# A two-layer graph network on one core: two more PSUM banks for the products of the list, and one table of columns

## The chip, the core and the metric

The kernel runs on one core of one Trainium2 chip. The metric is the device time of one execution in microseconds; the kernel before has a median of 3094.66 us over 3 runs (3094.16 to 3096.91). The engines have the names of the profile: PE is TensorE (PEld its weight loads), DVE is VectorE, ACT is ScalarE, POOL is GpSimd, SP is SyncE.

## The reference

The input is a graph with 12500 nodes of 128 features and 200000 edges sorted by target. Each edge has a relation, 0 to 9, the argmax of ten of its attributes. A layer takes for each target node and relation the mean of the source nodes' features, multiplies it by that relation's 128 x 128 matrix, sums over relations, and adds the node's own features times a root matrix and a bias:

```python
seg = dst * NUM_REL + edge_type
sums = segment_sum(x[src], seg, N * NUM_REL)
cnt = segment_sum(ones, seg, N * NUM_REL)
mean = (sums / maximum(cnt, 1)[:, None]).reshape(N, NUM_REL, -1)
layer = einsum('nrd,rdo->no', mean, w_rel) + x @ root + bias
```

There are two such layers, with a relu between them. The result is the layer norm of x plus the second layer's output.

## The kernel before

Edges are handled in tiles of 128. For a tile, POOL gathers the 128 source rows from DRAM (`gathered`, L749). DVE builds a one-hot matrix, 128 edges by (relation, node within a window of w nodes), by comparing a table of column numbers with one key per edge (`ones`, L757). ACT scales it by each edge's weight (`weighted`, L755). PE multiplies the gathered rows by the one-hot (the placement product, L976 in layer 1 and L1479 in layer 2) into a PSUM bank. DVE adds the bank into `cc`, a ring of sums in SBUF, at an offset read from a register (`sum_into`, L790). When all edges of a block of nodes are in, PE projects the block: ten products with the relations' matrices and one with what is there already (`projected`, L737 and L740). ACT copies it (L1413), PE transposes it (L1420), and DVE and ACT normalise it and store it (`normed`, L698 to L710). ACT clears the ring behind it (`cleared`, L720), and at the start of each lap of the ring DVE adds its overhang into it (`folded`, L727).

Layer 1 goes through all edges and, for edges whose source is finished already, does layer 2's share as well. What is left for layer 2 is, first, 166 tiles at the start (the plain bunches), and then a list of the edges that layer 1 had to skip. The list is put together on the chip during the plain bunches (`brought_together`, `listed`), in `mask`, a PSUM tile with the name "go" of three banks, and in one half of the ring, which is cleared again afterwards; from then on `ready` holds "ring". The list has 709 tiles.

In layer 2 a bunch is one product bank: several tiles of the same window, or one tile, or one piece of at most 48 of a wider window (up to 120 nodes). The loop at L1450 writes every engine's order out by hand (nothing is rescheduled). Iteration p issues:

- the one-hot of bunch p+4 on DVE (AH is 4) and the weighting of bunch p+3 on ACT. There are six one-hot buffers, so a one-hot waits for the product six bunches before its own;
- the gathers of bunch p on POOL, eight rows of tiles to a buffer, with seven buffers (GB);
- the products of bunch p on PE, into a bank of the pool `ps_y`, which has three;
- due steps of the list's making;
- the additions of bunch p-2 on DVE (BE is 2);
- if a block is now complete, its projection; and the later steps of earlier blocks (transposes, normalisation, clearing) that are due by the count of tiles gathered. Once all tiles are gathered, a block's steps follow each other at once.

The eight PSUM banks are: two for projections and transposes (`ps_f`), three for the products (`ps_y`), three for `mask`. After the list is built, `mask` holds three tables of column numbers (for pieces that begin at columns 0, 48 and 96) and small helpers.

Waits between engines come from the framework: an instruction waits for the earlier ones whose tile it overwrites or reads.

Of the kernel before, what the change touches and what calls it, by code (L numbers as in the profile page):

```python
# [9 lines left out]
F32 = mybir.dt.float32  # L10
# [3 lines left out]
ALU = mybir.AluOpType  # L14
# [6 lines left out]
P = 128  # L21
NREL = 10
EMB = 16
RS = 32
WN = 12
KW = NREL * WN
WZ = 48
WMAX = 120
# [14 lines left out]
YB = 512  # L43
# [20 lines left out]
def rgcn_resnorm_kernel(ctx: ExitStack, tc: tile.TileContext, x, src, dst, attr, w_rel1, root1, b1,  # L64
# [7 lines left out]
    nc = tc.nc  # L72
# [35 lines left out]
    def finished_in(k):  # L108

        return -(-done_after(k) // QB) - 1 + BEHIND  # L110
# [4 lines left out]
    ER = RT * P  # L115
# [3 lines left out]
    for k in range(K0, K1 + 1):  # L119
        r = max(0, -(-(QB * (finished_in(k) + READY) - T0) // RT))  # L120
# [33 lines left out]
    def rows_at(u, at):  # L154

        rs = [r for r, (lo, hi) in at.items() if lo < u * P + P and hi > u * P]
        return (min(rs), max(rs)) if rs else (max(at), max(at))
# [7 lines left out]
    for l, (a, last) in enumerate(((0, SPLIT), (SPLIT, NR))):  # L165
        while a < last:
            b = a + 1
# [9 lines left out]
            a = b  # L177
# [55 lines left out]
    def chunk_rows(c):  # L233
        return min(CT, NT - c * CT)
# [109 lines left out]
    n = chunk_rows(NCH - 1)  # L344
# [402 lines left out]
    def gathered(g, j, table, idx, n):  # L747

        nc.gpsimd.indirect_dma_start(out=g[:, j * C:(j + n) * C], out_offset=None, in_=table,  # L749
                                     in_offset=bass.IndirectOffsetOnAxis(ap=idx, axis=0))  # L750

    def weighted(oh, j, m, w):

        s = oh[:, j * m:(j + 1) * m]
        nc.scalar.activation(s, s, AF.Copy, scale=w)  # L755

    def ones(keys, cols, n, w):  # L757

        oh = dpool.tile([P, YB], F32, name="oh")
        m = NREL * w  # L760
        o = oh[:, :n * m]
        if w == WN:
            nc.vector.tensor_tensor(o.rearrange("p (t m) -> p t m", m=m), cols[:, None, :m].to_broadcast([P, n, m]),  # L763
                                    keys[:, :, None].to_broadcast([P, n, m]), op=ALU.is_equal)
        else:
            nc.vector.tensor_tensor(o.rearrange("p (t r n) -> p t r n", r=NREL, n=w),  # L766
                                    cols[:, None, :, :w].to_broadcast([P, n, NREL, w]),
                                    keys[:, :, None, None].to_broadcast([P, n, NREL, w]), op=ALU.is_equal)
        return oh

    def offsets(row, t0, n, limits):
# [270 lines left out]
    ps_y = fast.enter_context(tc.tile_pool(name="ps_y", bufs=3, space=PSUM))  # L1042
# [7 lines left out]
    mask = ps_m.tile([P, 3 * YB], I32, name="go")  # L1050
    iotaM = mask[:, P + ER - KW:P + ER].bitcast(F32)
    nc.vector.tensor_copy(iotaM, columns[:, :KW])
    tables = {WN: iotaM}
# [3 lines left out]
    def brought_together(ready, first):  # L1057

        EW = P + ER
# [19 lines left out]
        tri, wide = flat[:, at:at + P], flat[:, at + P:at + P + NREL * WZ].rearrange("p (r n) -> p r n", n=WZ)  # L1079
# [15 lines left out]
        for a in range(0, RT, 4):  # L1095
            pt = ps_f.tile([P, YB], F32, name="pf")
            n = min(RT - a, 4)
# [43 lines left out]
        for s in range(11):  # L1141
# [11 lines left out]
            c = max(m, KW)  # L1153
# [8 lines left out]
        for a, b, t in ((0, KW, gl[:, :KW]), (KW, EW, go)):  # L1162
            q = t.bitcast(F32)
# [2 lines left out]
            nc.vector.scalar_tensor_tensor(v[:, a:b], d0[:, a:b], 0.5, q, op0=ALU.is_gt, op1=ALU.mult)  # L1166
        nc.vector.scalar_tensor_tensor(A, d0, 0.5, A, op0=ALU.is_gt, op1=ALU.mult)
        yield 1
        for c in range(0, WMAX, WZ):
            w = min(WZ, WMAX - c)  # L1170
            t = mask[:, c * NREL:(c + w) * NREL].bitcast(F32).rearrange("p (r n) -> p r n", n=w)
            nc.vector.tensor_scalar(t, wide[:, :, :w], float(c), None, op0=ALU.add)
            tables[c, WZ] = t
        assert WMAX * NREL <= ER
        n = -(-NT2 // P)
        assert sorted(first) == list(range(n))
        hots = [t[:, :EW].rearrange("r (c t) -> r c t", t=P) for t in (X, Y)]
# [2 lines left out]
        def put(i, c):  # L1180

            u0, u1 = c * P, min(NT2, c * P + P) - 1
            p = u1 + 1 - u0
            m = max(-(-(P - 1 + cap_of[r]) // P) for r in range(rows_at(u0, extent[u0 >= UX])[0], rows_at(u1, extent[u1 >= UX])[1] + 1))
            assert m * P <= EW
            o = WMAX * NREL + i * (EW // P)
            assert o + EW // P <= EW - KW
            qc = mask[:, o:o + EW // P].bitcast(F32)
            nc.vector.tensor_scalar(qc[:NR, :m], columns[:NR, :m], f[:NR, 3:4], -float(u0), op0=ALU.add, op1=ALU.add)
            hot = hots[i % 2]  # L1190
            nc.vector.tensor_tensor(hot[:, :m], columns[:NR, None, :].to_broadcast([NR, m, P]),
                                    qc[:NR, :m, None].to_broadcast([NR, m, P]), op=ALU.is_equal)
            pp = ps_f.tile([P, YB], F32, name="pf")
            for j in range(m):
                nc.tensor.matmul(pp[:p, :2 * P], hot[:, j, :p], both[:, :, j * P:(j + 1) * P], start=(j == 0), stop=(j == m - 1))  # L1195
            nc.scalar.activation(packed[:p, c], pp[:p, :2 * P], AF.Copy)

        put(0, first[0])
        yield 1
        head = listed(first[0])  # L1200
# [87 lines left out]
    def layer_2():  # L1288
# [16 lines left out]
        bunches = [(0, False, t, min(QB, T0 - t), WN, 0, WN) for t in range(0, T0, QB)]  # L1305
# [135 lines left out]
        busy = 0  # L1441
        flag = None
        gs, ohs, zps, offs = {}, {}, {}, {}
        AH, BE = 4, 2
        i = 0
        ready = set()
        wanted = list(dict.fromkeys(c for _, second, t0, n, *_ in bunches if second for c in (t0 // P, (t0 + n - 1) // P)))
# [2 lines left out]
        for p in range(-AH, NB + BE):  # L1450
            if p + AH < NB:
                l, second, t0, n, w, c, _ = bunches[p + AH]
                keys = keyB if second else keyE
                assert not second or {t0 // P, (t0 + n - 1) // P} <= ready
                ohs[p + AH] = ones(keys[:, t0:t0 + n], tables[(c, WZ) if second else WN], n, w)
            if 0 <= p + AH - 1 < NB:
                l, second, t0, n, w, c, _ = bunches[p + AH - 1]
                for j in reversed(range(n)):
                    weighted(ohs[p + AH - 1], j, NREL * w, (wB if second else wE)[:, t0 + j:t0 + j + 1])
            if p == -AH:  # L1460
                jobs.run(0)
            if p < 0:
                continue
            if p < NB:
                l, second, t0, n, w, c, whole = bunches[p]
                oh = ohs.pop(p)
                zp = zps[p] = ps_y.tile([P, YB], F32, name="zp")
                if not c:
                    for j in range(n):
                        if made % GQ == 0:  # L1470
                            g = gpool.tile([P, GQ * C], F32, name="g")
                        gs[second, t0 + j] = g, made % GQ
                        made += 1
                        idx = (idxB if second else idxE)[:, t0 + j:t0 + j + 1]
                        gathered(g, gs[second, t0 + j][1], hD, idx, 1)
                m = NREL * w
                for j in range(n):
                    gt, b = gs[second, t0 + j]
                    nc.tensor.matmul(zp[:, j * m:(j + 1) * m], gt[:, b * C:(b + 1) * C], oh[:, j * m:(j + 1) * m],  # L1479
                                     start=True, stop=True)  # L1480
                    if c + w == whole:
                        del gs[second, t0 + j], gt
                i = issued[p + 1]
            if flag is None and i >= NG - 8 * QB:
                flagged()
                flag = 0
            jobs.run(i)
            q = p - BE
            if q >= 0:
                l, second, t0, n, w, c, whole = bunches[q]  # L1490
                assert not l or "ring" in ready
                for j in range(n):
                    t = t0 + j
                    if (second, t) not in offs:
                        if second:
                            m = min(GB2, (UX, NT2)[l] - t)
                            assert {t // P, (t + m - 1) // P} <= ready
                            vals = offsets(rowB[:, t:t + m], t, m, bounds2)
                        else:
                            m = min(GB2, T0 - t)  # L1500
                            if t % CT == 0:
                                row = rows_.tile([1, CT], I32, name="row")
                                nc.scalar.dma_start(row, b_i[t // CT:t // CT + 1, :])
                            vals = offsets(row[:, t % CT:t % CT + m], t, m, bounds)
                        offs = {k: v for k, v in offs.items() if k[0] and (k[1] >= UX) != l}
                        offs.update({(second, t + d): v for d, v in enumerate(vals)})
                    ring = 1 - l
                    sum_into(slice(ring, ring + 1), zps[q], j * NREL * w, offs[second, t], w, c)
                del zps[q]
            while due and due[0][0] <= q + 1 and (i >= busy or i >= NG or clear[due[0][1]] and i + 2 >= free_until(due[0][1])):  # L1510
                k = due.pop(0)[1]
                finish(k, i)
                ended.add(k)
                busy = i + (13 if block(k)[1] > YB * 5 // 8 else 9)
            todo.run(i)
# [173 lines left out]
```

## Time and profile before

| | |
|---|---|
| median of 3 runs | 3094.66 us |
| profiled execution: time, span | 3098.4 us, 3096.6 us |
| mean granted TensorE clock | 0.823 |
| PE busy | 2427.0 us, 78% |
| DVE busy | 1989.1 us, 64% |
| ACT busy | 1292.9 us, 42% |
| POOL busy | 2308.9 us, 75% |
| first gather of layer 2 | 1971.1 us |
| last gather | 3065.2 us |

Times in the profile are counted from the start of the span. Busy time leaves out register and semaphore work and the issuing of DMAs. Each row of a group has the line, engine, operation and shapes, then busy time, mean ns of one, and the idle time of its engine just before it, with what ended it; "issue" there means that the profile names no cause. A row of a timeline has the start, the time taken and, in brackets, the idle time before it. A row of a stretch has its bounds and length, the busy time and count of each engine in it (PE, PEld, DVE, ACT, POOL in this order, those that have any), the granted TensorE clock, the share of the DMA engines, and GB/s. An fp32 product shows as two PE records.

### The profile page before, as it was taken

How to read it: one execution, taken by the hardware profiler on the slowest of the kernel's cores; microseconds unless marked ns; L12 is line 12 of the kernel's file. 1: busy time of each engine (PE TensorE's matmuls, PEld its weight loads, DVE VectorE, ACT ScalarE, POOL GpSimd, SP SyncE). 2: the span in 40 equal slices, each digit the busy share in tenths (PEclk: the TensorE clock that was granted, in tenths of full speed). 3: DMA queues.
4: the chain of work that ended last, by engine and by line, in shares of the span. 5: the costliest groups of instructions: out<-in, count | busy, mean ns of one | idle time of the engine just before them, and what ended most of it. 6: DMA issues, size and time to landing. Idle time of an engine off the chain costs nothing.

```text
span 3096.6 us, 39943 instructions
## 1 busy us (share of the span) xinstructions
PE 2427.0 (78%) x10905; PEld 1805.4 (58%) x10905; DVE 1989.1 (64%) x5272; ACT 1292.9 (42%) x3006; POOL 2308.9 (75%) x2450
## 2 busy tenths in 40 slices
PE   2768887888888888888888899646577787777887
PEld 2546666566666566666666667545555555555665
DVE  7875746465656565555555554598677677677676
ACT  3543333333333333333333334322445555555453
POOL 7777777777777777777777777677777777777774
PEclk8768888888888878787888789856788999988888
DMA  7865445454545454545454444322222222222222
GB/s 210 233 204 173 143 124 159 120 163 123 163 119 163 121 162 124 162 123 162 123 161 124 127 121 120 101 58 63 60 70 74 73 74 74 74 74 73 74 73 59
DMA packets 260631, 371.57 MB, mean 120 GB/s; under 512 B 49654, under 2 KB 189467, under 8 KB 260404
## 3 DMA queue, kind: packets, MB, share of 16 engines
q0 software_dynamic: 100368, 251.49, 29.5%
q1 hardware_dynamic: 106339, 91.83, 9.6%
q10 hardware_dynamic: 53697, 25.62, 2.8%
q8 instruction: 94, 1.54, 0.2%
q14 instruction: 133, 1.09, 0.1%
HBM read 323.78 MB, written 57.76 MB: 123 GB/s over the span
## 4 chain that ended last, share of the span: by engine, by line
PE 37%; POOL 18%; issue 16%; DVE 13%; DMA 11%; ACT 3%; DVEq 1%; ACTq 0%; POOLq 0%; SPq 0%
POOL g L749 18%; PE pf L737 16%; DMA g<-XH,idxE 10%; PE zp L976 9%; PE zp L1479 8%; DVE cc L790 4%; DVE oh L766 2%; PE pf L740 1%; ACT cc L720 1%; ACT oh L755 1%; DVE cc L1157 1%; PE pf L1195 1%; DVEq L775 1%; DVE oh L763 1%; DVE go L1145 1%
## 5 line engine op out<-in xcount | busy, mean ns | idle before, releaser
L749 POOL DMA_INDIRECT g<-XH,idxE x1397 | 1321.7, 946 | 425.6 <-issue 383.9
L790 DVE TENSOR_TENSOR cc<-cc,zp 128x240 f32 (+16 forms) x2507 | 962.9, 384 | 719.7 <-PE zp L976 503.1
L976 PE MATMUL zp<-oh,g 128*128 128x120 f32 x5920 | 1053.4, 334 | 323.6 <-DMA g<-XH,idxE 230.5
L976 PEld LDWEIGHTS zp<-oh,g 128*128 128x128 f32 x5920 | 926.1, 236 | 482.4 <-issue 187.1
L749 POOL DMA_INDIRECT g<-hD,idxB x709 | 670.2, 945 | 216.1 <-issue 202.7
L755 ACT ACTIVATE oh<-oh,wE 128x120 f32<-128x120 f32 x1729 | 530.2, 383 | 640.8 <-DVE oh L763 557.3
L1479 PE MATMUL zp<-oh,g 128*128 128x120 f32 (+18 forms) x1888 | 514.8, 417 | 256.8 <-DVE cc L790 102.3
L737 PE MATMUL pf<-cc,w 128*128 128x256 f32 (+6 forms) x2120 | 691.4, 485 | 30.3 <-DVE cc L790 21.3
L1479 PEld LDWEIGHTS zp<-oh,g 128*128 128x128 f32 x1888 | 346.1, 230 | 401.8 <-issue 252.2
L737 PEld LDWEIGHTS pf<-cc,w 128*128 128x128 f32 x2120 | 411.8, 208 | 279.6 <-issue 205.0
L755 ACT ACTIVATE oh<-oh,wB 128x150 f32<-128x150 f32 (+18 forms) x778 | 342.6, 483 | 293.7 <-DVE oh L766 276.6
L766 DVE TENSOR_TENSOR oh<-go,keyB 128x480 f32<-128x480 f32 (+14 forms) x478 | 262.9, 550 | 132.8 <-PE zp L1479 131.6
L720 ACT ACTIVATE cc<-zero 128x2560 f32<-128x2560 f32 (+4 forms) x188 | 322.0, 1717 | 21.7 <-DVE cc L790 19.6
L763 DVE TENSOR_TENSOR oh<-bank,keyE 128x480 f32<-128x480 f32 x391 | 253.2, 648 | 0.0
L670 ACT ACTIVATE a<-pf,b 128x512 f32<-128x512 f32 (+1 forms) x27 | 17.3, 639 | 453.6 <-PE pf L740 453.6
L749 POOL DMA_INDIRECT g<-hD,idxE x166 | 158.4, 954 | 62.6 <-issue 46.6
L749 POOL DMA_INDIRECT g<-in_x_dram,idxE x166 | 157.0, 946 | 52.3 <-issue 47.2
L546 DVE TENSOR_TENSOR eqb<-bank,kh 128x1344 bf16<-128x1344 f32 (+2 forms) x65 | 100.5, 1549 | 2.3 <-PE pf L557 1.9
L555 PE MATMUL pf<-eqb,identb 128*128 128x512 bf16 (+2 forms) x130 | 64.7, 498 | 11.6 <-DVE eqb L546 11.4
L882 ACT ACTIVATE v<-pf,b 128x512 f32<-128x512 f32 (+2 forms) x29 | 18.0, 619 | 120.1 <-PE pf L740 100.5
L557 PE MATMUL pf<-eqb,identb 128*128 128x512 bf16 (+2 forms) x130 | 64.1, 493 | 0.0
L415 DVE SCALAR_TENSOR_TENSOR reach<-u,reach 128x6 f32<-128x6 f32 x252 | 42.2, 167 | 7.4
(235 smaller groups left out, 991.5 us busy)
## 6 DMA issues: line engine op xcount, KB each, us to landing
m<-in_edge_attr_dram SPq DMA_DIRECT2D x48, 672.0 KB
g<-XH,idxE POOLq DMA_INDIRECT x1397
XH<-in_x_dram ACTq DMA_DIRECT2D x24, 512.0 KB
XH<-zero ACTq DMA_DIRECT2D x24, 512.0 KB
g<-hD,idxB POOLq DMA_INDIRECT x709
XH<-hb SPq DMA_DIRECT2D x43, 256.0 KB
out_dram<-o SPq DMA_DIRECT2D x47, 128.0 KB
xb<-in_x_dram SPq DMA_DIRECT2D x23, 256.0 KB
```

Of the source, the lines that this page charges most:

```text
L546: nc.vector.tensor_tensor(eq[:p], kpP[:p, None, :R].to_broadcast([p, DB, R]), fore, op=ALU.is_equal)
L555: nc.tensor.matmul(pc[:p], identb[:p, :p], eq[:p, k:k + 4, L:], start=(d + k == 1), stop=False)
L557: nc.tensor.matmul(pc[:p], identb[:p, :p], back, start=False, stop=(d + k + 3 == L))
L720: nc.scalar.activation(cc[:, l, h * H:(h + 1) * H, o:o + n], zero[:, None, :n].to_broadcast([P, H, n]), AF.Copy)
L737: nc.tensor.matmul(po[:, :n], wsb[l][:, r, :], cc[:, l if ring is None else ring, r, o:o + n], start=(r == 0), stop=False)
L749: nc.gpsimd.indirect_dma_start(out=g[:, j * C:(j + n) * C], out_offset=None, in_=table, in_offset=bass.IndirectOffsetOnAxis(ap=idx, axis=0))
L755: nc.scalar.activation(s, s, AF.Copy, scale=w)
L763: nc.vector.tensor_tensor(o.rearrange("p (t m) -> p t m", m=m), cols[:, None, :m].to_broadcast([P, n, m]), keys[:, :, None].to_broadcast([ ...
L766: nc.vector.tensor_tensor(o.rearrange("p (t r n) -> p t r n", r=NREL, n=w), cols[:, None, :, :w].to_broadcast([P, n, NREL, w]), keys[:, :, ...
L790: nc.vector.tensor_tensor(s, s, z, op=ALU.add)
L976: nc.tensor.matmul(zp[:, a + l * KW:a + (l + 1) * KW], g[:, (slot[j] + l) * C:(slot[j] + l + 1) * C], oh[:, j * KW:(j + 1) * KW], start=Tr ...
L1479: nc.tensor.matmul(zp[:, j * m:(j + 1) * m], gt[:, b * C:(b + 1) * C], oh[:, j * m:(j + 1) * m], start=True, stop=True)
```

## The change

In the list part, once "ring" is ready, bunches go around five banks in place of three: those with p % 5 of 3 or 4 use the second and third bank of `mask`. The additions of the list are issued three bunches behind the products (BE is 3), those of the plain bunches two behind as before. So that the two banks are free, one table of 48 columns, in the first bank of `mask`, replaces the three: for a piece that begins at column c, the one-hot's comparison adds c in the same instruction (a scalar-tensor-tensor form in place of the tensor-tensor form).

```diff
-    def ones(keys, cols, n, w):
+    def ones(keys, cols, n, w, c=0):
...
-            nc.vector.tensor_tensor(o.rearrange("p (t r n) -> p t r n", r=NREL, n=w),
-                                    cols[:, None, :, :w].to_broadcast([P, n, NREL, w]),
-                                    keys[:, :, None, None].to_broadcast([P, n, NREL, w]), op=ALU.is_equal)
+            to = o.rearrange("p (t r n) -> p t r n", r=NREL, n=w)
+            a = cols[:, None, :, :w].to_broadcast([P, n, NREL, w])
+            b = keys[:, :, None, None].to_broadcast([P, n, NREL, w])
+            if c:
+                assert n == 1
+                nc.vector.scalar_tensor_tensor(to[:, 0], a[:, 0], float(c), b[:, 0], op0=ALU.add, op1=ALU.is_equal)
+            else:
+                nc.vector.tensor_tensor(to, a, b, op=ALU.is_equal)
...
-        for c in range(0, WMAX, WZ):
-            w = min(WZ, WMAX - c)
-            t = mask[:, c * NREL:(c + w) * NREL].bitcast(F32).rearrange("p (r n) -> p r n", n=w)
-            nc.vector.tensor_scalar(t, wide[:, :, :w], float(c), None, op0=ALU.add)
-            tables[c, WZ] = t
-        assert WMAX * NREL <= ER
+        assert WZ * NREL <= YB
+        tables[WZ] = mask[:, :WZ * NREL].bitcast(F32).rearrange("p (r n) -> p r n", n=WZ)
+        nc.vector.tensor_copy(tables[WZ], wide)
...
-            o = WMAX * NREL + i * (EW // P)
+            o = WZ * NREL + i * (EW // P)
...
-        AH, BE = 4, 2
+        AH, BE = 4, 3
+        plain = sum(not b[1] for b in bunches)
...
-                ohs[p + AH] = ones(keys[:, t0:t0 + n], tables[(c, WZ) if second else WN], n, w)
+                ohs[p + AH] = ones(keys[:, t0:t0 + n], tables[WZ if second else WN], n, w, c)
...
+            five = p >= plain and "ring" in ready
...
-                zp = zps[p] = ps_y.tile([P, YB], F32, name="zp")
+                if p % 5 > 2 and five:
+                    b = p % 5 - 2
+                    zp = mask[:, b * YB:(b + 1) * YB].bitcast(F32)
+                else:
+                    zp = ps_y.tile([P, YB], F32, name="zp")
+                zps[p] = zp
...
-            q = p - BE
-            if q >= 0:
+            q = p - (BE if five else BE - 1)
+            if q in zps:
```

## The prediction

> **What bounds the kernel now.** I began with the busy time by stretches, to see where the changed code runs: the list part of layer 2, from about 2200 us to the end. Then came the waits of the stretch 2250 to 3065, then its groups, then the timeline of a few bunches and of the end. The first four rows below are busy times by stretch; the last two count, from the first gather of layer 2 to 2500 us, the gathers and the records of the placement products. A row of waits gives total us, times, and longest us.
>
> ```profile
> 2000.00:2100.00 100.00, 46.92 (x199) 40.08 (x197) 95.97 (x172) 29.83 (x83) 75.93 (x80) 0.61 0.23 60
> 2100.00:2200.00 100.00, 64.16 (x291) 54.68 (x291) 72.02 (x179) 38.02 (x98) 75.69 (x80) 0.74 0.23 58
> 2300.00:2500.00 200.00, 159.63 (x573) 103.17 (x571) 140.64 (x379) 108.00 (x208) 151.24 (x161) 0.91 0.28 73
> 2250.00:3065.00 815.00, 645.07 (x2510) 466.72 (x2511) 586.74 (x1624) 433.04 (x894) 616.39 (x652) 0.89 0.28 73
> 1971.00:2500.00 529.00, 400.28 (x423) 0.77 0.27 70
> 1971.00:2500.00 529.00, 218.89 (x806) 148.42 (x806) 0.77 0.27 70
> ```
> ```profile
> POOL g L749 <- issue: 186.2, 611, 0.3
> DVE oh L766 <- PE zp L1479: 129.0, 52, 6.2
> PE zp L1479 <- issue: 59.0, 25, 3.1
> PE zp L1479 <- DVE cc L790: 52.7, 39, 4.8
> DVE cc L790 <- PE pf L737: 35.2, 8, 5.8
> PE zp L1479 <- DMA g<-hD,idxB: 4.1, 6, 1.1
> ```
> ```profile
> L1479 PE MATMUL zp<-oh,g 128*128 128x150 f32 (+16 forms) x1471 | 424.7, 427 | 156.3 <-issue 59.0 <-DVE cc L790 52.7 <-PE zp L1479 12.8
> L766 DVE TENSOR_TENSOR oh<-go,keyB 128x480 f32<-128x480 f32 (+15 forms) x462 | 253.4, 548 | 130.2 <-PE zp L1479 129.0 <-PE pf L1230 0.3
> L737 PE MATMUL pf<-cc,w 128*128 128x256 f32 (+4 forms) x860 | 209.0, 402 | 16.9 <-DVE cc L790 8.4 <-DVE cc L727 8.2
> ```
>
> POOL issues gathers at an even pace (616.39 us busy plus 186.2 us of 0.3 us gaps in 815), so it looks like the bound. But the products do not keep up with it: up to 2500 us there are 423 gathers and 806/2 = 403 products, two records each, so PE is 20 gathers (25 us) behind, and it waits for a gather only 4.1 us in all. The seven g buffers hold 56 gathers, so this lag holds nobody; it decides the end, though, because PE must still work it off. What PE and DVE do together is therefore the chain of this part. POOL is a floor close beneath it.
>
> DVE waits for PE 129.0 + 35.2 = 164.2 us. There are 860/20 = 43 projections of a block and 462 bunches, so one block is 815/43 = 18.95 us, 10.7 bunches, and 3.8 us of DVE waiting. Nearly all the waiting lies behind a projection, as these rows show: the projection, the first product after it, and the one-hot it releases.
>
> ```profile
> 2606.46 5.81 PE L737 MATMUL pf<-cc,w 128*128 128x256 f32 x20
> 2612.53 1.96 PE L1479 MATMUL zp<-oh,g 128*128 128x480 f32 x10
> 2613.54 0.66 DVE L766 TENSOR_TENSOR oh<-go,keyB 128x480 f32<-128x480 f32 x1 [5.30 <-PE zp L1479]
> ```
>
> Elsewhere DVE runs without a pause. DVE's own work is thus 18.95 - 3.8 = 15.1 us per block; with about 3 us for a block's normalisation (3.1 in the rows of the end below), one iteration of DVE is (15.1 - 3)/10.7 = 1.13 us. Two kinds of iteration, one-hot and additions, in rows: 1.29 us with two tiles of 24 columns, 1.44 with three of 15.
>
> ```profile
> 3041.90 0.65 DVE L766 TENSOR_TENSOR oh<-go,keyB 128x480 f32<-128x480 f32 x1
> 3042.47 0.81 DVE L790 TENSOR_TENSOR cc<-cc,zp 128x230 f32 x2
> 3043.19 0.65 DVE L766 TENSOR_TENSOR oh<-go,keyB 128x480 f32<-128x480 f32 x1
> ...
> 2603.64 0.62 DVE L766 TENSOR_TENSOR oh<-go,keyB 128x450 f32<-128x450 f32 x1
> 2604.17 0.99 DVE L790 TENSOR_TENSOR cc<-cc,zp 128x150 f32 x3
> 2605.08 0.65 DVE L766 TENSOR_TENSOR oh<-go,keyB 128x480 f32<-128x480 f32 x1
> ```
>
> **The change, part by part.** One table: three operations that wrote 480, 480 and 240 columns become one copy of 480; each took 0.58 us, so about 1.2 us of DVE goes, once, in the stage that builds the list. I take it as nothing: bounds 0 and -1.2 us. For pieces beyond the first (69 of them: 944 products for 875 gathers), the one-hot adds its offset in a scalar-tensor-tensor form. No such row of 480 elements exists; the nearest has 1408 in 1675 ns, or 0.57 for 480 if proportional, against 0.65 for the plain form. Bounds 69 x (-0.08 to +0.08) = -6 to +6 us; I take 0, as it is the same work per element.
>
> ```profile
> L1172 DVE TENSOR_SCALAR go<-cc 128x480 f32<-128x480 f32 (+1 forms) x3 | 1.7, 578 | 0.1
> L1103 DVE SCALAR_TENSOR_TENSOR cc<-cc,seen_below,go 127x1408 f32<-127x1408 int32 x1 | 1.7, 1675 | 0.0
> ```
>
> Five banks, additions three behind. By the text of the kernel, the product of bunch p now needs the addition of p-5 where it needed p-3, and the 52.7 us (and probably the 59.0 us without a named cause) of PE's waits would shrink. But the two added banks are cut from the tile "go", whose first bank holds the table that every one-hot reads, and the built order of the changed kernel shows what that makes of the waits. Of 190 products into these two banks, 188 wait for the one-hot of p+4, issued just ahead of them; and where the bunch before wrote into one of these banks, the one-hot of p+4 waits for the product of p-1 (185 times) where it waited for p-2. So in two iterations of each five DVE and PE run in lock step: one-hot, product, one-hot. Nothing in the banks demands this, but it is in the program.
>
> One lock step costs DVE: one-hot 0.65, then 0.09 until the product starts (addition's end 3052.18 + 0.83, product at 3053.10), then 1.02 from the product's start to the next one-hot (3060.84 to 3061.86), 1.76 in all where the iteration lasted 1.29: 0.47 us. With three tiles of 15: 0.62 + 0.09 + 1.02 - 1.44 = 0.29. I take 0.4.
>
> ```profile
> 3052.18 0.83 DVE L790 TENSOR_TENSOR cc<-cc,zp 128x240 f32 x2
> 3053.10 1.94 PE L1479 MATMUL zp<-oh,g 128*128 128x240 f32 x4 [2.75 <-issue]
> 3060.84 2.59 PE L1479 MATMUL zp<-oh,g 128*128 128x240 f32 x12
> 3061.86 0.66 DVE L766 TENSOR_TENSOR oh<-go,keyB 128x480 f32<-128x480 f32 x1 [4.10 <-PE zp L1479]
> ```
>
> Per block, of 10.7 iterations three fall behind the projection and one behind the normalisation, where the wait is hidden; 6.7 x 2/5 x 0.4 = 1.07 us remain. Behind the projection, DVE could do two iterations before it ran out of one-hot buffers. With the new waits this depends on where in the five the block ends: in two of five positions one of these iterations (1.13) must wait until after the projection, in one of them with a lock (0.4) on top, and in one position DVE must await a second product (424.7/462 = 0.92). That is (1.13 + 1.53 + 0.92)/5 = 0.72. Sum 1.79 us per block.
>
> How well does such counting do? For the block above, projection start to one-hot is 7.08 us, less two iterations of 1.13 gives 4.8; the row has 5.30, but the mean over blocks is 3.8. So I take 0.8 of the sum: 1.43 x 43 = 62 us. From below: if lead won elsewhere eats half, 30; from above: unscaled 1.79 x 43 = 77, with full locks also behind normalisations and projections (190 x 0.47 = 89).
>
> The end of the kernel:
>
> ```profile
> 3065.15 0.94 POOL L749 DMA_INDIRECT g<-hD,idxB  x1 [0.30 <-issue]
> 3068.20 2.72 DVE L790 TENSOR_TENSOR cc<-cc,zp 128x240 f32 x6
> 3069.12 4.50 PE L1479 MATMUL zp<-oh,g 128*128 128x240 f32 x12 [3.26 <-issue]
> 3073.46 4.88 PE L737 MATMUL pf<-cc,w 128*128 128x280 f32 x20
> 3078.65 0.97 PE L1479 MATMUL zp<-oh,g 128*128 128x240 f32 x4
> 3079.46 0.49 PE L1420 MATMUL pf<-ident,a 128*128 128x128 f32 x3
> 3080.42 0.60 DVE L698 TENSOR_TENSOR v<-pf,xb 128x256 f32<-128x256 f32 x2
> 3080.55 4.65 PE L737 MATMUL pf<-cc,w 128*128 128x260 f32 x20 [0.60 <-DVE cc L790]
> 3082.67 0.85 DVE L708 TENSOR_SCALAR o<-v,mv,rstd 128x128 f32<-128x128 f32 x3
> ```
>
> Now the last projection (3080.55) starts 7.1 us after the one before it. In the changed order that earlier projection comes after the last product, and its normalisation stands on DVE ahead of the additions of the last three bunches, on which the last projection waits: 6.5 (to the end of the transposes, 3079.95) + 3.1 (3080.42 to 3083.52) + 2.72 (three bunches) = 12.3, 5.2 more. The last product ahead of it adds 0.97; the 3.26 us wait for a bank falls away. Sum +3 us.
>
> The order on POOL and SP is the same line for line; layer 1 and the list's making are too, but for the table.
>
> Together 62 + 3 = 65 us. The profiled execution took 3098.4 us for its span of 3096.6, 3.7 above the median of 3094.66. From the median: 3160 us.
>
> **The rivals.** First, not slower: PE's greater lead frees the chain, the bank waits go (52.7 + 59.0 us of PE), the lag behind the gathers vanishes, and POOL sets the end. Then the last product can end no sooner than the last gather's end (3066.1) + 2.5 us of landing + 0.97, and the last projection follows 12.3 + 0.1 later, near 3082, 1.4 us after today's: about 3096, no change. It cannot be much faster, as POOL's row leaves no gap to win.
>
> ```profile
> 2539.73 2.48 DMA g<-hD,idxB
> ```
>
> It decides if DVE's waits fall below those of today by over half a microsecond a block; against it stands that they already lie behind projections, which no bank shortens.
>
> Second, half: the locks hide in pauses that the lead opens, and only what lies behind the projections and the end stays: 0.72 x 43 = 31, +3: 3129 us.
>
> Third, the clock. The granted clock goes with PE's busy share: 0.61 at 47%, 0.74 at 64%, 0.89 at 79%. Stretched by 62 us, the list part has 645/877 = 74% and by these rows about 0.84, so the projections' 209 us grow by 0.89/0.84, 12 us, and the products, where they lock, by some 10 more: 3182 us.
>
> The Trainium skill, "TensorE: Matmul & The Clock Gate", section "A second HAM failure mode: psum-queue depth-cycling", says that a kernel cycling through PSUM banks with short idle moments between groups of matmuls has its clock throttled again and again. The rows agree in direction: less busy, lower clock. By that rule the third rival is the likely one, by the steady 0.89 of the rows mine is.
>
> **How the numbers follow.** Forecast (locks, clock as now) 0.48; half 0.20; clock 0.18; not slower 0.10; something faster, by lead that I fail to see, 0.04. A measurement of this kernel can tell 0.2%, 6 us. The range runs from 3108, below the half case less its unknowns of some 20 us, to 3195, the clock case with full locks. Slower 0.86, same 0.10, faster 0.04.
>
> **What would show it.** Right: one-hots (the plain line of the list) that wait for products twice as often, in short waits of about half a microsecond; products into "go" that wait for a one-hot; PE over 25 us behind the gathers and POOL at last waiting for a free buffer; a last gather well before the end. Wrong: DVE's waits at or below 164 us in the list part, POOL even to the end and an end near 3096; or a granted clock well below 0.84.

## The result, and the profile after

The changed kernel takes 3236.78 us, median of 5 runs (3235.52 to 3238.52), against 3094.66 (3094.07 to 3097.15) before: a ratio of 1.0458, 95% interval 1.0442 to 1.0473. It is 142 us slower. The forecast was slower, 3160 us with a range to 3195; the direction holds, the size is more than double and the time lies outside the range.

The loss lies in the list part alone. These are the busy times by stretch (bounds and length, then PE, PEld, DVE, ACT, POOL with their counts, granted clock, DMA share, GB/s), first of the kernel before, then of the changed one:

```profile
0.00:1970.00 1970.00, 1608.61 (x7610) 1191.66 (x7611) 1171.99 (x3075) 753.93 (x1818) 1480.28 (x1575) 0.82 0.51 148
1970.00:2250.00 280.00, 155.95 (x718) 133.63 (x716) 216.36 (x523) 101.71 (x283) 211.27 (x222) 0.67 0.27 69
2250.00:3200.00 950.00, 662.39 (x2579) 480.09 (x2579) 600.79 (x1676) 437.25 (x906) 617.34 (x653) 0.90 0.25 64
```
```profile
0.00:1970.00 1970.00, 1600.33 (x7609) 1185.16 (x7610) 1171.25 (x3074) 754.00 (x1817) 1480.66 (x1575) 0.82 0.50 148
1970.00:2250.00 280.00, 155.21 (x719) 132.49 (x718) 216.03 (x519) 101.61 (x283) 211.09 (x222) 0.67 0.27 69
2250.00:3200.00 950.00, 692.45 (x2521) 497.73 (x2521) 598.80 (x1641) 437.70 (x900) 617.11 (x654) 0.84 0.24 63
```

Up to 2250 us the two are the same, also in counts: by that time the same number of gathers has been issued. From there DVE, ACT and POOL do the same work as before within 2 us; only it takes about 140 us longer. So what grew is waiting. The waits of the changed kernel from 2250 us to the end (total us, times, longest):

```profile
DVE oh L773 <- PE go L1488: 181.9, 121, 6.9
PE go L1488 <- DVE oh L773: 75.7, 44, 8.3
POOL g L749 <- PE zp L1488: 49.4, 29, 7.5
PE go L1488 <- ACT oh L755: 48.3, 31, 5.0
DVE oh L773 <- PE zp L1488: 43.1, 12, 5.2
POOL g L749 <- PE go L1488: 36.0, 12, 7.8
DVE oh L771 <- PE go L1488: 18.7, 18, 4.1
DVE oh L771 <- PE zp L1488: 18.4, 5, 5.6
PE go L1488 <- DVE oh L771: 21.7, 12, 4.3
PE zp L1488 <- DVE cc L795: 15.7, 10, 2.5
PE go L1488 <- DVE cc L795: 4.2, 5, 1.2
```

The one-hots (L773 and L771) wait for products 181.9 + 43.1 + 18.7 + 18.4 = 262.1 us in 156 waits; before it was 129.0 us in 52. The waits of a product for an addition have gone from 52.7 to 15.7 + 4.2 us: the added banks do give that. But the products into "go" now wait 75.7 + 21.7 us for a one-hot and 48.3 us for a weighting, and POOL, which nobody held for over 0.3 us before, waits 49.4 + 36.0 us for a gather buffer.

This is the wait that costs, in rows of the timeline of the changed kernel (start, time taken, idle time before it):

```profile
2718.43 0.34 DVE L771 SCALAR_TENSOR_TENSOR oh<-go,keyB 128x180 f32<-128x180 f32 x1
2718.69 0.64 DVE L795 TENSOR_TENSOR cc<-cc,zp 128x480 f32 x1
2718.82 1.97 PE L1488 MATMUL go<-oh,g 128*128 128x480 f32 x2 [2.87 <-DVE oh L771]
...
2720.83 0.66 DVE L773 TENSOR_TENSOR oh<-go,keyB 128x480 f32<-128x480 f32 x1 [1.50 <-PE go L1488]
2721.41 0.33 DVE L795 TENSOR_TENSOR cc<-cc,zp 128x180 f32 x1
2721.54 0.97 PE L1488 MATMUL go<-oh,g 128*128 128x180 f32 x2 [0.75 <-DVE oh L773]
...
2722.55 0.66 DVE L773 TENSOR_TENSOR oh<-go,keyB 128x480 f32<-128x480 f32 x1 [0.81 <-PE go L1488]
```

One-hot, product, one-hot, product, one-hot: each starts where the other engine's ends. Counted over the list part from the timeline's one-hot rows, waits of 0.5 to 2 us go from 9 (6.2 us) to 101 (95.4 us), and waits of over 2 us, those behind a projection, from 30 (118.5 us) to 35 (159.9 us). DVE does the same work as before, so its waits add to the time: 89 + 41 = 130 us.

At the end of the changed kernel:

```profile
3203.59 4.88 PE L737 MATMUL pf<-cc,w 128*128 128x280 f32 x20
...
3213.11 0.82 DVE L795 TENSOR_TENSOR cc<-cc,zp 128x240 f32 x2
3213.97 1.72 DVE L795 TENSOR_TENSOR cc<-cc,go 128x240 f32 x4
3215.74 7.04 PE L737 MATMUL pf<-cc,w 128*128 128x260 f32 x20 [5.70 <-DVE cc L795]
```

The last projection starts 12.15 us after the one before it, where it was 7.09 (3073.46 to 3080.55), and takes 7.04 us in place of 4.65: another 7.5 us. With the 130 that makes 138 of the 142 us.

### The profile page after: what moved, and what is told of

Read it like the earlier page. It is cut to its first block, busy times and chain, and to the rows that moved or that the text cites. A ratio compares the mean times of both kernels' runs of the same rounds, so it can differ in the third digit from the quotient of the medians.

```text
span 3233.7 us, 39802 instructions
## 1 busy us (share of the span) xinstructions
PE 2465.2 (76%) x10905; PEld 1828.5 (57%) x10905; DVE 1995.8 (62%) x5270; ACT 1295.3 (40%) x3006; POOL 2308.8 (71%) x2450
## 3 DMA queue, kind: packets, MB, share of 16 engines
q14 instruction: 133, 1.09, 0.1%
## 4 chain that ended last, share of the span: by engine, by line
PE 35%; POOL 18%; issue 16%; DVE 15%; DMA 12%; ACT 3%; DVEq 1%; ACTq 0%; POOLq 0%; SPq 0%
POOL g L749 18%; PE pf L737 15%; DMA g<-XH,idxE 11%; PE zp L981 9%; PE go L1488 5%; DVE cc L795 4%; PE zp L1488 3%; DVE oh L773 2%; ACT oh L755 1%; PE pf L740 1%; DVE cc L1162 1%; ACT cc L720 1%; DVE oh L763 1%; DVE st L701 1%; DVEq L780 1%
## 5 line engine op out<-in xcount | busy, mean ns | idle before, releaser
L795 DVE TENSOR_TENSOR cc<-cc,zp 128x240 f32 (+10 forms) x2198 | 839.1, 382 | 678.0 <-PE zp L981 503.5
L981 PEld LDWEIGHTS zp<-oh,g 128*128 128x128 f32 x5920 | 921.4, 235 | 492.1 <-issue 176.2
L737 PE MATMUL pf<-cc,w 128*128 128x256 f32 (+6 forms) x2120 | 708.7, 495 | 35.1 <-DVE cc L795 24.8
L737 PEld LDWEIGHTS pf<-cc,w 128*128 128x128 f32 x2120 | 426.7, 215 | 290.7 <-issue 205.3
L1488 PE MATMUL zp<-oh,g 128*128 128x120 f32 (+16 forms) x1270 | 330.9, 411 | 124.7 <-DVE cc L795 60.8
L1488 PE MATMUL go<-oh,g 128*128 128x150 f32 (+16 forms) x618 | 219.9, 478 | 209.5 <-DVE oh L773 75.7
L773 DVE TENSOR_TENSOR oh<-go,keyB 128x480 f32<-128x480 f32 (+12 forms) x409 | 234.2, 573 | 232.9 <-PE go L1488 187.5
L1488 PEld LDWEIGHTS zp<-oh,g 128*128 128x128 f32 x1270 | 245.7, 240 | 192.5 <-issue 136.3
L1488 PEld LDWEIGHTS go<-oh,g 128*128 128x128 f32 x618 | 115.4, 230 | 290.3 <-DVE oh L773 85.6
L795 DVE TENSOR_TENSOR cc<-cc,go 128x150 f32 (+16 forms) x309 | 123.5, 400 | 20.7 <-PE pf L737 9.2
L555 PE MATMUL pf<-eqb,identb 128*128 128x512 bf16 (+2 forms) x130 | 62.1, 477 | 12.0 <-DVE eqb L546 11.8
```

The costliest lines, as they stand in the source:

```text
L555: nc.tensor.matmul(pc[:p], identb[:p, :p], eq[:p, k:k + 4, L:], start=(d + k == 1), stop=False)
L737: nc.tensor.matmul(po[:, :n], wsb[l][:, r, :], cc[:, l if ring is None else ring, r, o:o + n], start=(r == 0), stop=False)
L773: nc.vector.tensor_tensor(to, a, b, op=ALU.is_equal)
L795: nc.vector.tensor_tensor(s, s, z, op=ALU.add)
L981: nc.tensor.matmul(zp[:, a + l * KW:a + (l + 1) * KW], g[:, (slot[j] + l) * C:(slot[j] + l + 1) * C], oh[:, j * KW:(j + 1) * KW], start=Tr ...
```

## The experiments

Three theories stood at the start, with the letters that the expectations use. L: the one-hots read a table that lies in the same tile "go" as the added banks, so one-hots and products wait for each other; without that sharing nearly all of the 142 us goes. B: the cost is in the later additions. C: more banks lower the clock, whoever shares them; the cost stays when the sharing goes.

**The parts one by one.** The changed kernel with the one table, but neither the added banks nor the later additions; with all but the later additions; with only one of the two added banks:

```diff
-            five = p >= plain and "ring" in ready
+            five = False
```


> Edit: the changed kernel with three banks and additions two behind; only the one table of columns, with the added offset, is left of the change. Theory L: 3095 us, within 6. Theory T (the scalar-tensor-tensor form is dear): 69 one-hots of this form would have to cost 2 us each for the whole loss; anything above 3110 us speaks for a share of it.

```diff
-            q = p - (BE if five else BE - 1)
+            q = p - (BE - 1)
```


> Edit: the changed kernel, five banks, but additions two behind everywhere. Theory L: the waits through the shared tile are all still there, so 3215 to 3245 us. Theory B (the later additions cost the time): back to 3095 to 3130 us.

```diff
-                if p % 5 > 2 and five:
-                    b = p % 5 - 2
+                if p % 4 > 2 and five:
+                    b = p % 4 - 2
```


> Edit: the changed kernel with four banks (one of them in the shared tile) in place of five; additions three behind. Theory L: one-hots that wait for the product just before are 117 in place of 185, so by proportion 3095 + 142 x 117/185 = 3185 us, between 3160 and 3205. If the number of banks as such or the lag of the additions costs the time, 3220 us or more.

The kernel before stood at 3095.81 us beside these. The table alone: 3095.39 us, ratio 1.0002 (0.9992 to 1.0012). It costs nothing, nor does the comparison that adds an offset: in the changed kernel its 69 instructions take 425 ns on average. Additions two behind: 3235.54 us, ratio 1.0453 (1.0435 to 1.0470), as slow as the whole change, so theory B falls. One added bank: 3172.15 us, ratio 1.0246 (1.0228 to 1.0263). Its short waits of one-hots are 62 (54.3 us), its long ones 148.0 us: 48 + 30 = 78 us more than before, for a loss of 76 us. With two added banks and additions two behind, the same count (100 short waits, 102.0 us; long ones 145.1) gives 122 of 140 us.

**The table out of the shared tile, first into SBUF.** Six gather buffers in place of seven make the room for it.

```diff
-GB = 7
+GB = 6
+    own_table = comp.tile([P, NREL, WZ], F32, name="own_table")
-        tables[WZ] = mask[:, :WZ * NREL].bitcast(F32).rearrange("p (r n) -> p r n", n=WZ)
+        tables[WZ] = own_table
```


> Edit: the table of columns gets an SBUF tile of its own, so that the two added banks share a tile with nothing that the one-hots read; to make room, six g buffers in place of seven. Theory L (the shared tile's waits cost the time): products into the added banks no longer wait for one-hots nor one-hots for the product just before; DVE's short waits (0.5 to 2 us, 99 of them in the changed kernel) go, the granted clock in the list part is back near 0.89, and the time is near POOL's floor, 3090 to 3100 us. Theory B (additions three behind, or five banks as such, cost the time): over 3180 us. Theory C (a slower PE clock by going around more banks is the cause, not the waits): clock stays near 0.84 and the time over 3150 us.

It takes 3134.77 us, ratio 1.0125 (1.0108 to 1.0142): 103 of the 142 us are gone, with both banks and the later additions in place. Theory L expected 3090 to 3100 us, so some 35 us more are left than it allows. Short one-hot waits are down to 25 (28.0 us). Its waits and its group of list gathers:

```profile
DVE oh L773 <- PE zp L1489: 73.7, 31, 5.9
DVE oh L773 <- PE go L1489: 49.5, 26, 5.3
PE zp L1489 <- DMA g<-hD,idxB: 40.8, 54, 1.9
PE go L1489 <- DMA g<-hD,idxB: 29.9, 47, 1.3
```
```profile
L749 POOL DMA_INDIRECT g<-hD,idxB x709 | 701.8, 990 | 216.1 <-issue 185.0
```

Now PE waits for the gathers, which it did for only 4.1 us before; and a gather takes 990 ns on average where it took 945. Forty microseconds stay, in a new place. Two causes for the longer gathers were open, the table in SBUF and the sixth buffer; below, the table's place is changed with the buffers left at seven, and the table is put into SBUF without any added bank.

**The table in a PSUM bank of its own.** Once the list is made, the tile `mask` is given up; one bank holds the table, and the added products get a pool of two banks. Call it the split kernel. It has seven gather buffers, and nothing else is changed in its list part. Three of its runs were on chips on which the kernel before itself took 3964 to 3968 us (more below); this one is on a chip like that of the other runs. In its expectation, S is that a table in SBUF lengthens the gathers, and F that five banks or the later additions themselves cost some 40 us.

```diff
+        building.close()
+        ps_t = fast.enter_context(tc.tile_pool(name="ps_t", bufs=1, space=PSUM))
+        added.append(fast.enter_context(tc.tile_pool(name="ps_q", bufs=2, space=PSUM)))
+        tab = ps_t.tile([P, YB], F32, name="tab")
+        tables[WZ] = tab[:, :WZ * NREL].rearrange("p (r n) -> p r n", n=WZ)
...
-                    b = p % 5 - 2
-                    zp = mask[:, b * YB:(b + 1) * YB].bitcast(F32)
+                    zp = added[0].tile([P, YB], F32, name="zq")
```


> The split kernel once more, for a chip on which the kernel before takes some 3095 us. Theory L+S: 3092 to 3105 us, gathers of the list at 945 to 948 ns, last gather near 3066. Theory F: 3125 to 3140 us.

3106.70 us, ratio 1.0036 (1.0022 to 1.0050): 130 of the 142 us gone. Theory L holds, in the strict form: the same five banks, the same late additions, no sharing. One thing changes along with it: `mask` is an int32 tile and the added banks were fp32 views of it, where the tiles of the split kernel are fp32 from the start. Whether the banks of an fp32 tile would have been kept apart was not tried. The short one-hot waits are 6 (7.0 us), fewer than before the change, and the gathers are back to 946 ns. Waits of this kernel from 2250 us on:

```profile
DVE oh L773 <- PE zp L1493: 58.4, 18, 6.7
DVE oh L773 <- PE zq L1493: 42.3, 13, 5.6
PE zp L1493 <- DVE cc L795: 34.0, 21, 2.9
PE zp L1493 <- DMA g<-hD,idxB: 24.3, 32, 2.6
```

Theory C does not account for the loss. The 900 projections of this stretch take 237.5 us here, against 238.0 in the changed kernel and 218.5 before, so PE runs them as slowly as there, and yet the list part is as long as before: the last gather starts at 3066.93 us (before: 3065.15). The reverse was seen too: with additions two behind they take 228.4 us, and the time is that of the changed kernel. The granted clock of the whole stretch, however, is 0.88 here (and 0.90 in the kernel of the next experiment, also with five banks), where it was 0.84 in the changed kernel and 0.90 before, and the products into the two added banks are faster than in the changed kernel. The rows are the stretch of the split kernel, then these products in the changed kernel and in the split one:

```profile
2250.00:3200.00 950.00, 672.04 (x2563) 487.85 (x2562) 594.64 (x1668) 435.98 (x903) 618.87 (x654) 0.88 0.25 64
...
L1488 PE MATMUL go<-oh,g 128*128 128x140 f32 (+17 forms) x594 | 213.8, 480 | 203.6 <-DVE oh L773 75.7 <-ACT oh L755 48.3 <-issue 34.4
...
L1493 PE MATMUL zq<-oh,g 128*128 128x480 f32 (+17 forms) x582 | 180.7, 438 | 41.5 <-DVE cc L795 15.8 <-DMA g<-hD,idxB 11.2 <-ACT oh L755 5.6
```

Without the shape 128x140, of which 12 records are missing in the split kernel, the same products take 207.2 us shared and 177.2 us apart. So 30 us of slower products come and go with the sharing. Which part of them lies in the waits of the one-hots, and whether the lower clock alone makes them slower, was not separated.

What stays is the end:

```profile
3070.98 2.15 PE L1493 MATMUL zq<-oh,g 128*128 128x240 f32 x4 [1.54 <-DMA g<-hD,idxB]
3072.92 5.51 PE L737 MATMUL pf<-cc,w 128*128 128x280 f32 x20
...
3082.30 0.85 DVE L708 TENSOR_SCALAR o<-v,mv,rstd 128x128 f32<-128x128 f32 x3
3083.08 0.82 DVE L795 TENSOR_TENSOR cc<-cc,zp 128x240 f32 x2
...
3085.71 7.37 PE L737 MATMUL pf<-cc,w 128*128 128x260 f32 x20 [5.70 <-DVE cc L795]
```

**The order at the end.** The same kernel, but a block's later steps no longer become due at once when all tiles are gathered, so the last additions stand ahead of the normalisation of the last block but one:

```diff
-            u = (1 if n > YB * 5 // 8 else 0.7) if i < NG else 0
+            u = 1 if n > YB * 5 // 8 else 0.7
```


> The split kernel (3106.7 us against 3095 before), with the last additions put ahead of the normalisation of the last block but one. If the order at the end makes the 12 us that are left, 3 to 8 us go: 3098 to 3104 us, and the end after the last gather shrinks from 38 us towards the 31.5 us of before. If the 12 us lie in the list part itself (the last gather of split came 1.8 us later than before), nothing goes: 3105 to 3108 us.

3097.25 us over 11 runs, ratio 1.0006 (0.9997 to 1.0015): no difference from before. The order at the end makes 9 of the 12 us that were left, a little more than expected. Its end, and its waits for gathers:

```profile
3064.92 0.94 POOL L749 DMA_INDIRECT g<-hD,idxB  x1 [0.31 <-issue]
...
3070.15 1.17 PE L1493 MATMUL zq<-oh,g 128*128 128x240 f32 x2 [0.27 <-DMA g<-hD,idxB]
3071.11 6.86 PE L737 MATMUL pf<-cc,w 128*128 128x280 f32 x20
...
3079.38 4.55 PE L737 MATMUL pf<-cc,w 128*128 128x260 f32 x20
```
```profile
PE zp L1493 <- DMA g<-hD,idxB: 20.1, 31, 2.1
PE zq L1493 <- DMA g<-hD,idxB: 17.2, 26, 1.9
```

Here five banks do what they can: PE follows the gathers so closely that the last product starts at 3070.15 us, 8.5 us earlier than the 3078.65 of before. Nothing is won by it. POOL issues its last gather when it did before, and the projection that follows runs at 6.86 us in place of 4.88, so the last one starts 1.2 us earlier than before.

**Is POOL the floor under the kernel before?** That kernel, three banks and three tables, with one-hots six ahead and eight one-hot buffers (six gather buffers for the room):

```diff
-GB = 7
-OB = 6
+GB = 6
+OB = 8
-        AH, BE = 4, 2
+        AH, BE = 6, 2
```


> The kernel before with its one-hots prepared six products ahead, additions two behind, six gather buffers and eight one-hot buffers; still three banks and separate tables. If POOL's gathers are the floor of the list part, the gain is small: 3086 to 3093 us. If the deeper buffers only move the waits, 3094 to 3097 us; if six gather buffers in place of seven hold POOL, 3098 to 3110 us.

3094.30 us over 11 runs, ratio 0.9998 (0.9989 to 1.0007). More lead for DVE and one gather buffer less change nothing together, and a list gather takes 948 ns, so the sixth buffer is not what made the gathers longer.

**The table in SBUF, three banks.** The kernel with its own table, without the added banks:

> Three banks, but the one table in a tile of its own in SBUF, six gather buffers. If the table in SBUF slows each list gather from 945 to 990 ns, 709 gathers take 32 us more and this kernel stands at 3118 to 3135 us though it has no added bank. If six gather buffers or the two added banks made the gathers of the kernel with its own table long, the gathers stay at 945 ns and it stands at 3093 to 3100 us.

3125.03 us, ratio 1.0102 (1.0086 to 1.0117), with gathers of 988 ns: 709 x 43 ns = 30 us, and 30 us is what it loses. The rest of the kernel with its own table, 9 us, is the size of the order at the end. Rows of the timeline show where a gather becomes long:

```profile
2453.38 0.94 POOL L749 DMA_INDIRECT g<-hD,idxB  x1 [0.30 <-issue]
...
2454.59 0.62 DVE L773 TENSOR_TENSOR oh<-own_table,keyB 128x450 f32<-128x450 f32 x1
2454.63 1.39 POOL L749 DMA_INDIRECT g<-hD,idxB  x1 [0.30 <-issue]
```

**On other chips.** Three sets of runs were on chips on which the kernel before takes 3964 to 3968 us; their sizes are not compared with the others. The work of the engines is nearly the same there: in the split kernel DVE is busy 1991.2 us against 1985.4, and POOL 2308.2 against 2310.5. The idle time is longer. DVE's additions wait 587.7 us for what the profile calls "remote", another core or an unknown queue, a cause that it names nowhere in the split kernel on the chip like the others. What it is stays open. The expectations give times for chips like the first, so only their order can be read here.

> Edit: once the list is put together the tile of three banks is given back, and its banks become a tile with the table alone and a pool of two for the added products; the table stays in PSUM and seven g buffers stay. (The last plain one-hots read the columns from SBUF.) Theory L+S (shared-tile waits cost the 142 us; the 39 us that were left with the table in SBUF are gathers slowed by DVE's reads of SBUF): gathers of the list at 945 ns, as before, and the time at POOL's floor, 3092 to 3100 us. Theory G (six g buffers caused the 39 us) gives the same time here, so the run with three banks and the SBUF table tells these two apart. Theory F (five banks or the later additions themselves cost some 40 us): 3125 to 3140 us.

> Edit: as the run with split tiles, and at the end, when all tiles are gathered, the steps of the last block but one are kept until the last block's projection is due, so that the last additions stand on DVE ahead of its normalisation. Theory L with the prediction's working of the end (normalisation 3.1 us ahead of the additions costs the last projection some 5 us): 3 to 6 us less than the split run, 3088 to 3094 us, just under the kernel before. If that order is hidden: the same as the split run within 2 us.

> Edit: the kernel before the change with one-hots six bunches ahead and eight one-hot buffers (in place of four and six), and six g buffers to make room. Theory D (behind a projection DVE stops because it runs out of one-hot buffers, 129 us of waits in the list part): these waits halve, the lag behind the gathers vanishes, and the time falls to POOL's floor, 3086 to 3092 us. If the banks hold the chain anyway: 3093 to 3098 us. If six g buffers hold POOL: POOL waits for PE by more than 0.3 us at a time.

> Edit: three banks and additions two behind, as before the change, with the one table in an SBUF tile of its own and six g buffers. Theory S (DVE's reads of the table from SBUF slow POOL's gathers): the gathers of the list take about 990 ns in place of 945, 30 us in all, and the time is 3120 to 3135 us. Theory G or F: gathers at 945 ns; G then has POOL waiting for buffers, F gives 3095 us.

There the kernel with the table in its own bank gave ratios of 0.9935, 0.9914 and 0.9934 on three such chips, with the other end 0.9908 and 0.9911, the kernel before with more lead 0.9767 and 0.9773, the table in SBUF with three banks 0.9729 and 0.9727 (intervals of about 0.003 either way). So on such chips the order changes. Both kernels of the last two pairs have six gather buffers, and start layer 2 earlier than the split kernels there (first gather at 2421 to 2429 us against 2481 to 2496); whether the buffers do that, or something that comes with them, was not separated, and none of it shows on the chips of the other runs. Beside the changed kernel itself:

> The split kernel (table alone in one PSUM bank, two banks for the added products, seven g buffers), third time. On a chip where the kernel before takes some 3095 us: theory L+S 3092 to 3105 us with gathers of the list at 945 to 948 ns and a last gather near 3066; theory F 3125 to 3140 us. On the slow chip: 3925 us, as before.

> The changed kernel as it is, on the same chip as the split kernel. On a chip like the first: 3237 us. On the slow chip theory L expects it well above the split kernel there, by 142 us or more, since each lock step has two waits between engines, and these are longer on that chip; theory F expects both within 40 us.

3934.70 us against 4002.27 us, so the sharing costs 68 us there, with the changed kernel at 1.0100 (1.0077 to 1.0123). That is less than half of the 142 us or more that were expected, and not within theory F's 40 either. The reason given for more, longer waits between engines, does not show in a direct step: from ACT's root (L704) to DVE's reciprocal (L705) it takes 0.04 us at the median there and 0.03 on the other chip. Why the loss is smaller was not found.

## Why the prediction was right in kind and short in size

**What bounds the kernel.** The prediction said: PE and DVE together are the chain, POOL a floor close beneath. The floor is confirmed, closer than it was put: with the locks gone and PE hard behind the gathers, the time is 3097 us, and with more lead on three banks 3094. So the prediction was wrong to call PE and DVE the chain: they did not hold the kernel before by any amount that can be measured; PE's lag of 20 gathers cost nothing but the last 8 us of products, which the end swallows.

**One table, scalar-tensor-tensor: nothing.** Right: 1.0002 (0.9992 to 1.0012).

**Five banks: false waits through the tile "go".** Right in mechanism and nearly in number. 6.7 x 2/5 locks a block in 43 blocks is 115; 92 more short waits were counted. Undoing the sharing alone takes 130 of the 142 us away.

**"I take 0.4" for one lock: this is the step that failed.** The added short waits are 89.2 us / 92 = 0.97 us each. The working took the length of an iteration (1.29 and 1.44) from two rows with bunches of two and three tiles, and subtracted it from a cycle made of another bunch's product. But one-hot, product and addition of an iteration belong to three bunches. In the rows above, the product at 2721.54 releases the one-hot at 2722.55, 1.01 us later, as priced; the addition that fills this time takes 0.33, not 0.81, so the wait is 0.81 us. And the product at 2718.82, into 480 columns, takes 1.97 us and holds the next one-hot for 1.50 us. Over all 101 short waits both terms are off. From the start of one one-hot to the start of the next, which waited, it takes 2.04 us on average, where the working put 1.76 and 1.73; without the wait it would be 1.09, where it put 1.29 and 1.44. The 266 iterations of the stretch that hold only additions and no such wait last 1.07 us without their waits, so the two chosen rows were long ones, and the prediction's own mean, 1.13, was closer. Of the missing 0.57 us, about 0.3 is thus the longer cycle, and nearly as much the shorter work beside it. Which part of the longer cycle is from slow products was not separated.

**"So I take 0.8 of the sum".** It went the wrong way: by it the locks were 1.07 x 43 x 0.8 = 37 us, where 89 were found, and the waits behind projections 0.72 x 43 x 0.8 = 25 us, where 41 were found: 62 in all, for 130. The factor came from waits that lie behind a projection, and was put on waits that do not.

**The end, +3 us.** The 12.3 us between the last two projections came out at 12.15. What was missed is that the last one then takes 7.04 us, for 4.65, after a longer idle time of PE; and the order at the end, measured by itself, is worth 9 us.

**The rivals.** "Not slower", POOL sets the end at 3096 us, is just what the banks do without the sharing and with the old order at the end: 3097.25. "Half" was wrong by its sign: the locks did not hide in pauses. "The clock" was right in its number, 0.84 in the list part for the forecast 0.84, though its time, 3182 us, is short as well, and the projections grew by 238.0 - 218.5 = 19.5 us. By the rule of the Trainium skill's "TensorE: Matmul & The Clock Gate", section "A second HAM failure mode: psum-queue depth-cycling", this was to be expected, and the rows agree in direction. But slow projections are not what cost the time: the kernel with the table in its own bank runs them as slowly, 237.5 us, and loses nothing in the list part. The products into the added banks grew by 30 us, not by some 10, and may be part of the lock's price.

**What would show it.** All signs named as "right" came: one-hots that wait, 156 times in place of 52 and 262 us in place of 129, though the short waits are of one microsecond and not half of one; products into "go" that wait for one-hots; PE 417 - 740/2 = 47 gathers behind at 2500 us, by the rows below of gathers and of product records since 1971 us; POOL held; and a last gather at 3139 us, 94 us ahead of the end, where it was 31.

```profile
1971.00:2500.00 529.00, 395.49 (x417) 0.74 0.27 68
...
1971.00:2500.00 529.00, 203.31 (x740) 141.73 (x740) 0.74 0.27 68
```

## What to carry to other kernels

Before a spare part of a tile is used as a buffer, look at who else reads that tile: in this kernel the waits went by the tile, not by the bank, so a table that every instruction of one engine reads ties that engine to each write into its neighbour bank, and two engines that ran side by side take turns. To price such a turn, take both the cycle of the two engines and the iteration that it replaces as means over the stretch, not from single rows; a lock is long where the work beside it is short. And more buffers win nothing above a floor: here POOL's pace of gathers decided, and neither banks nor lead could show a gain.

## What the hardware showed unexpectedly

A table of columns in SBUF lengthens POOL's gathers: 988 and 990 ns on average with the table in SBUF (983 and 981 on the other chips), 944 to 948 ns with it in PSUM on the chips of both kinds. The median stays at 944 ns; some gathers become long. In the kernel with three banks and the table in SBUF, from 2250 us on, the 421 list gathers that overlap a one-hot take 1.009 us on average, and 106 of them over 1 us; the 233 that overlap none take 0.947 us, with 2 over 1 us. In the kernel before, it is 0.942 and 0.945. The Trainium skill, "SBUF — State Buffer", section "Who interferes with whom", says that a VectorE instruction with two inputs in SBUF contends with a GpSimd instruction that reads SBUF. The runs agree: with the table in SBUF, both inputs of the comparison, table and keys, lie there; with it in PSUM, one does. That the contention is at this port, and not elsewhere in SBUF, no run here shows.
